# Channel sums of a state-space mixer: from image rows on chip instead of a read-back from DRAM

## The chip, the cores and the metric

The kernel runs on one core of one Trainium2 chip. The metric is device time in microseconds (us) of one execution. A core has TensorE (PE: matrix products and transposes), VectorE (DVE), ScalarE (ACT), GpSimd (POOL) and SyncE (SP, which here only issues DMAs). Each engine works through its own instructions in the order in which the program gave them; semaphores tie the engines and the DMAs together. An instruction that waits holds up everything behind it on its engine.

## The reference

Two layers run on two images of 128 channels and 64x64 pixels. Layer 0 has four deformable convolutions (60 taps, each gathers four neighbours per pixel), a fusing product and a small expert network. Layer 1 has a state-space mixer and another expert network. What the change touches is the channel and position attention in the mixer:

```python
xz = jnp.einsum('ed,bdhw->behw', in_proj_w, hidden_states)
xz = lax.conv_general_dilated(xz, dwconv_w, ..., feature_group_count=2 * DI)   # 5x5, one per channel
x, z = (xz[:, :DI], xz[:, DI:])                  # DI = 256 channels each, L = 4096 pixels
avg = jnp.mean(x, axis=-1, keepdims=True)        # per channel, over all pixels
mx = jnp.max(x, axis=-1, keepdims=True)
x = jax.nn.sigmoid(ca_branch(avg) + ca_branch(mx)) * x
stats = jnp.concatenate([jnp.mean(z, axis=1, ...), jnp.max(z, axis=1, ...)], axis=1)   # per pixel
att = lax.conv_general_dilated(stats, sa_conv_w, ...)
z = jax.nn.sigmoid(att) * z
```

After it come a causal convolution along the pixels, a scan (256 channels x 16 states x 4096 steps per image) and an output product. `ca_branch` is a product with a 16x256 matrix, a SiLU, and a product with a 256x16 matrix.

## The kernel before

**The large stages.** One instruction stream does layer 0 and the mixer for both images. The instructions of all engines are in an order that Python generators write out by hand. First come the 480 taps of image 0, then the 480 taps of image 1 (`sample`, line 755): per tap four indirect gathers on POOL (L748) into one of six buffers `v`, a weighting on DVE (L789, L791, L792), four transposes on PE into `pst`, a copy on ACT (L796) and the product on PE (L816), which is issued two taps late. Then comes the scan of image 0 (`scan`, line 1568), then that of image 1, then the last expert network. A scan has 256 units per image (8 pieces `k` of 512 pixels x 2 halves x 16 states). A unit is a scan on DVE (L1685) of `da` (ACT, L1604) and `db` (POOL, L1597, from a row `bcb` that SP loads, L1615), a transpose on PE (L120, `ht`), a weighting on DVE (L1631) and an adding transpose on PE (L1642).

**What runs beside them.** Everything between the taps of an image and its scan (fusing product, expert network, the mixer's convolutions) is a chain of generators, `after(b)`. For image 0 it runs beside the taps of image 1: each tap takes two steps of it (L806). For image 1 it runs beside the scan of image 0: each unit earns one credit, and steps are taken until it is spent (L1710). A step is charged what it yields, 0.11 where it yields nothing. So steps that are added or taken away shift all later side work against the units. When the side work of image 1 has ended, the remaining units of image 0 run alone, with half of the weighting on ACT, and from piece 7 on with the preparation of image 1's first piece (`prepare`, four of its steps per unit).

**The mixer's convolutions** (`convs`, line 1186) go through four groups `o` of 128 channels, in the order 2, 3, 0, 1: 2 and 3 are z, 0 and 1 are x. In each group comes first the input product (L1251, 22 steps charged 0.45; ACT copies the result to `X`). Then for two parts of 64 channels: the 5x5 convolution as products with position matrices (L1264, 8 steps; ACT copies to `Y`), and the image rows (L1286: PE transposes of `Y`; ACT copies into `img`; SP writes `img` to the DRAM tensors `xsd` or `zsd`). An `img` tile has 128 partitions, 64 channels of the upper and the same 64 channels of the lower half of each patch; four of them, `py` = 0 to 3, make up the 64 channels. They have three buffers, in a tag `io` that other tiles share. Copies are not issued at once: `later` holds them back by two steps, `last` issues what is held.

**The sums, before.** For z, DVE reduces all of `Y` over its 64 channels, once by adding (L1304) and once by the maximum (L1306), with one step between. For x, `channel_stats` (line 1337) loads the channels back from `xsd`, 128 partitions x 512 pixels at a time (L1340, 256 KB, 16 loads per image, in the `io` buffers), and reduces each load twice (L1343, L1344). The loads of the first 128 channels run beside the input product of group 1 (`at == 2`, L1311), those of the second after everything else (L1313). Then `channel_attention` (line 1347) combines eight partial results per channel and does the two small products (L1359, L1366), two sigmoids and the scaling of the taps' weights (L1370).

Of the kernel before, what the change touches and what calls it, by code (L numbers as in the profile page):

```python
# [10 lines left out]
F32 = mybir.dt.float32  # L11
I32 = mybir.dt.int32
AF = mybir.ActivationFunctionType
ALU = mybir.AluOpType
AX = mybir.AxisListType
# [4 lines left out]
P = 128  # L20
# [3 lines left out]
N = H * W  # L24
# [6 lines left out]
NG = NT // GT  # L31
# [1057 lines left out]
PH, PW = 8, 6  # L1089
# [3 lines left out]
NPOS = PH * PW  # L1093
CG = 128
YG = 64
# [36 lines left out]
class L1Conv:  # L1132
# [11 lines left out]
    def constants(self):  # L1144
        nc, d, wp = self.env.nc, self.env.d, self.wp

        def load(name, shape, src=None):
            t = wp.tile(shape, F32, name="w_" + name)
            nc.sync.dma_start(out=t, in_=d[name] if src is None else src)
            return t  # L1150

        self.c1w = load("conv1d_w", [P, 2, 4])
        self.c1b = load("conv1d_b", [P, 2])
        self.xpw = load("x_proj_w", [P, 2, 40])
        self.dtb = load("dt_proj_b", [P, 2])
        self.A = load("A_log", [P, 2, DS])
        self.D = load("D", [P, 2])
        self.fc1 = load("ca_fc1_w", [P, 2, 16])
        self.fc2 = load("ca_fc2_w", [16, 256])
        self.saw = load("sa_conv_w", [14, 1])  # L1160
        yield
        self.sqb = wp.tile([P, len(SQUARES)], F32, name="sqb")
        for i, (_, t, _) in enumerate(SQUARES):
            nc.vector.memset(self.sqb[:, i : i + 1], t)
        nc.scalar.activation(self.A, self.A, AF.Exp)
        nc.vector.tensor_scalar(self.A, self.A, -1.0, None, ALU.mult)
        self.xsd = [self.dp.tile([256, N], F32, name=f"xsd{b}", tag=f"xsd{b}") for b in range(B)]
        self.zsd = [self.dp.tile([256, N], F32, name=f"zsd{b}", tag=f"zsd{b}") for b in range(B)]
        self.att = [self.dp.tile([2, N + 6], F32, name=f"att{b}", tag=f"att{b}") for b in range(B)]
        self.sad = [self.dp.tile([1, N], F32, name=f"sad{b}", tag=f"sad{b}") for b in range(B)]  # L1170
        self.w1 = [wp.tile([P, 2, 4], F32, name=f"w1_{b}") for b in range(B)]
        for b in range(B):
            for s in range(2):
                nc.sync.dma_start(out=self.att[b][s : s + 1, 0:3], in_=self.env.zero[0:1, 0:3])
                nc.sync.dma_start(out=self.att[b][s : s + 1, N + 3 :], in_=self.env.zero[0:1, 0:3])
            yield
# [9 lines left out]
    def convs(self, b, sp, pp):  # L1186


        env, nc, d = self.env, self.env.nc, self.env.d
        bank = lambda shape, name: pp.tile(shape, F32, name=name, tag="m")  # L1190
# [9 lines left out]
        def last():  # L1200
            while held:
                for f in held.popleft():
                    f()
                yield 0.3
            yield
# [3 lines left out]
        hs, own, tm, beside = self.hs[b], {}, {}, deque()  # L1209
# [30 lines left out]
            matrices()  # L1240
        yield 0.5
        zst = sp.tile([NPATCH, 2, 256 // YG, NPOS], F32, name="zst", bufs=1)
        st = sp.tile([P, 2, 2, NG], F32, name="st8", bufs=1)
        for at, o in enumerate(ORDER):
            X = sp.tile([KP, CG, NPATCH], F32, name="X", bufs=1)
            for p0 in range(0, NPATCH, 4):
# [9 lines left out]
            for part in range(CG // YG):  # L1256
# [23 lines left out]
                for py in range(PH // 2):  # L1280
                    img = sp.tile([P, NI, W], F32, name="img", tag="io", bufs=3)
                    for x0, nx in ((0, 4), (4, 2)):
                        ps = bank([P, nx, NPATCH], "ps3")
                        for x in range(nx):
                            two = Y[:, py * PW + x0 + x, :, :].rearrange("p h c -> p (h c)")
                            nc.tensor.transpose(ps[:, x, :], two, env.ident[:NPATCH, :NPATCH])  # L1286
                        nj = NJ if x0 + nx <= W - PW * (NJ - 1) else NJ - 1
                        to = view(img, x0, [(W, NI), (PW, nj), (1, nx)])
                        todo = [copy(to, ps.rearrange("p x (i j) -> p i j x", j=NJ)[:, :, 0:nj, :])]
                        if x0:  # L1290
                            for h in range(2):
                                row = dst[:, py + h * PH // 2, :, :]
                                todo.append(functools.partial(nc.sync.dma_start, out=row, in_=img[h * YG : (h + 1) * YG]))
                        later(*todo)
                        yield 0.45
                    if py == 1:
                        matrices()
                        if part == 0:
                            weights(at + 1)
                yield from last()  # L1300
                if not x_half:
                    n = lo // YG
                    zs = zst[:, :, n, :].rearrange("p k (h s) -> p k s h", h=2)
                    nc.vector.tensor_reduce(zs[:, 0, :, :], Y, AX.X, ALU.add)  # L1304
                    yield
                    nc.vector.tensor_reduce(zs[:, 1, :, :], Y, AX.X, ALU.max)  # L1306
                yield
            if at == 1:
                beside.append(self.position_attention(b, zst, sp, bank, room))
            if at == 2:  # L1310
                beside.append(mixed([self.channel_stats(b, 0, g, st, sp) for g in range(NG)], 2))  # L1311

        yield from mixed([self.channel_stats(b, 1, g, st, sp) for g in range(NG)], 3)  # L1313
        yield from self.channel_attention(b, st, sp, bank)

    def norm(self, b, x, hn, g, sp, bank, banks, act):
# [17 lines left out]
        nc.scalar.copy(hs[:, 0 : NJ - 1, rows, PW : PW + 4], hs[:, 1:NJ, rows, 0:4])  # L1334
        yield

    def channel_stats(self, b, half, g, st, sp):
        nc = self.env.nc
        xs = sp.tile([P, 512], F32, name="xst", tag="io", bufs=3)
        nc.sync.dma_start(out=xs, in_=self.xsd[b][half * P : (half + 1) * P, g * 512 : (g + 1) * 512])  # L1340
        for _ in range(3):
            yield
        nc.vector.tensor_reduce(st[:, half, 0, g : g + 1], xs, AX.X, ALU.add)  # L1343
        nc.vector.tensor_reduce(st[:, half, 1, g : g + 1], xs, AX.X, ALU.max)  # L1344
        yield

    def channel_attention(self, b, st, sp, bank):

        nc = self.env.nc
        one = lambda shape, name: sp.tile(shape, F32, name=name, bufs=1)  # L1350
        amp = one([P, 2, 2], "amp")
        for half in range(2):
            nc.vector.tensor_reduce(amp[:, half, 0:1], st[:, half, 0, :], AX.X, ALU.add)
            nc.vector.tensor_reduce(amp[:, half, 1:2], st[:, half, 1, :], AX.X, ALU.max)
            nc.vector.tensor_scalar(amp[:, half, 0:1], amp[:, half, 0:1], 1.0 / N, None, ALU.mult)
        yield
        p1 = bank([16, 2], "p1")
        for half in range(2):
            nc.tensor.matmul(p1, self.fc1[:, half, :], amp[:, half, :], start=half == 0, stop=half == 1)  # L1359
        r1, r2 = one([16, 2], "r1"), one([16, 2], "r2")  # L1360
        nc.scalar.activation(r1, p1, AF.Sigmoid)
        nc.vector.tensor_tensor(r2, r1, p1, ALU.mult)
# [753 lines left out]
```

## Time and profile before

| what | value |
|---|---|
| median of three runs | 7552.04 us (7550.52 to 7557.68) |
| the profiled execution: its own time | 7555.38 us |
| the profiled execution: its span | 7553.5 us |
| busy DVE / PE / POOL / ACT in the span | 5857.3 / 5203.1 / 5036.0 / 2135.7 us |
| mean granted TensorE clock | 0.825 |
| mixer's convolutions of image 0, beside image 1's taps | 4216 to 5411 us |
| last tap of image 1 | 5722 us |
| scan of image 0 | 5764 to 6743 us |
| mixer's convolutions of image 1, beside it | 6198 to 6666 us |

The span runs from the first to the last instruction. A busy share is a mean over stages with different limits, so each stage has to be read for itself. In a list of waits a line names the instruction that waited, what ended the wait, and the total in us, the number of waits and the longest. In a line of the timeline stand the start and the duration in us, engine, line, operation, output and input; the number in brackets is the idle time of the engine just before, and what ended it. In a table of stretches stand busy us and, in brackets, the number of instructions of each engine, then the granted clock, the share of DMA time and GB/s.

### The profile page before, as it was taken

What the parts mean: (1) busy time and instruction counts of PE and PEld (TensorE: products, weight loads), DVE (VectorE), ACT (ScalarE), POOL (GpSimd) and SP (SyncE); (2) the same over time, 40 slices, a digit from 0 to 9 for tenths busy, and PEclk for the clock granted to TensorE, in tenths of its full rate; (3) what the DMA queues carried; (4) which work ended last, traced back from release to release, by engine and by line L of the source; (5) the groups of instructions that cost most, each with busy time, mean ns of one, the idle gap of its engine ahead of it and who ended that gap; (6) DMA issues with size and microseconds to landing.
All of it is one profiled execution on the core that took longest, in us unless ns stands there. A gap on an engine that the chain in (4) does not pass through costs nothing.

```text
span 7553.5 us, 71416 instructions
## 1 busy us (share of the span) xinstructions
PE 5203.1 (69%) x22497; PEld 3269.2 (43%) x22497; DVE 5857.3 (78%) x6710; ACT 2135.7 (28%) x4194; POOL 5036.0 (67%) x5062
## 2 busy tenths in 40 slices
PE   4666777777767675766666766666556788867668
PEld 3344444444444442333323444434223567755444
DVE  6878888888888887788888877777775787678782
ACT  2211111111111111311111121211114675667870
POOL 4666777777777777777777776677775445567850
PEclk7887887878888887888888887877777898888899
DMA  7886777776777767877777777687775334555444
GB/s 239 253 275 206 216 210 218 211 220 208 220 213 219 214 210 251 281 232 212 224 217 216 217 232 235 207 251 216 228 208 188 118 103 129 138 155 163 153 148 156
DMA packets 667316, 1550.02 MB, mean 205 GB/s; under 512 B 181668, under 2 KB 230988, under 8 KB 666940
## 3 DMA queue, kind: packets, MB, share of 16 engines
q0 software_dynamic: 307200, 1006.88, 44.2%
q1 hardware_dynamic: 332540, 492.98, 20.9%
q10 hardware_dynamic: 27200, 45.59, 1.6%
q8 instruction: 182, 2.98, 0.2%
q14 instruction: 194, 1.59, 0.1%
HBM read 1436.70 MB, written 110.84 MB: 205 GB/s over the span
## 4 chain that ended last, share of the span: by engine, by line
PE 39%; issue 18%; another core or an unknown queue 13%; DVE 8%; POOL 7%; ACT 7%; DMA 3%; SPq 1%; ACTq 0%; DVEq 0%; POOLq 0%
PE out L816 17%; PE pst L120 6%; POOL v L748 5%; PE po L437 4%; POOL db L1597 2%; DVE h L1685 2%; ACT st L796 2%; DVE v L789 2%; PE ps L1264 2%; PE pfo L892 1%; PE ps L1251 1%; PE px L1045 1%; PE ht L120 1%; DVE q L1557 1%
## 5 line engine op out<-in xcount | busy, mean ns | idle before, releaser
L748 POOL DMA_INDIRECT v<-table,idx x3840 | 4042.1, 1053 | 1629.6 <-issue 1047.7
L789 DVE TENSOR_TENSOR v<-v,pw 128x2048 f32<-128x2048 f32 x960 | 2192.0, 2283 | 611.3 <-DMA v<-table,idx 429.3
L816 PE MATMUL out<-st,regw 128*128 128x512 f32 x3840 | 2234.7, 708 | 225.3 <-issue 164.1
L796 ACT COPY st<-pst 128x512 f32<-128x512 f32 x960 | 556.9, 586 | 4402.2 <-remote 2198.4
L120 PE MATMUL pst<-ident,v 128*128 128x128 f32 x3840 | 721.3, 313 | 1061.0 <-issue 874.3
L791 DVE TENSOR_TENSOR v<-v 128x1024 f32<-128x1024 f32 x960 | 1177.3, 1226 | 33.0
L816 PEld LDWEIGHTS out<-st,regw 128*128 128x128 f32 x3840 | 790.7, 228 | 887.1 <-issue 813.5
L120 PEld LDWEIGHTS pst<-ident,v 128*128 128x128 f32 x3840 | 517.3, 161 | 1431.5 <-issue 1214.8
L1597 POOL TENSOR_TENSOR db<-du,bcb 128x512 f32<-128x512 f32 x512 | 670.9, 1311 | 493.5 <-DVE h L1685 382.8
L1685 DVE TENSOR_TENSOR_SCAN h<-da,state,db 128x512 f32<-128x512 f32 x512 | 651.8, 1273 | 77.9 <-ACT da L1604 48.0
L792 DVE TENSOR_TENSOR v<-v 128x512 f32<-128x512 f32 x960 | 664.2, 692 | 33.0
L120 PE MATMUL ht<-ident,h 128*128 128x128 f32 x2048 | 357.6, 303 | 221.0 <-ACT w L1633 150.9
L437 PE MATMUL po<-wa,win 128*128 128x147 f32 x2112 | 386.4, 306 | 104.7 <-issue 101.9
L437 PEld LDWEIGHTS po<-wa,win 128*128 128x128 f32 x2112 | 339.4, 204 | 226.6 <-issue 226.2
L1604 ACT ACTIVATE da<-delta,w_A_log 128x512 f32<-128x512 f32 x512 | 357.7, 699 | 262.6 <-DVE h L1685 258.0
L120 PEld LDWEIGHTS ht<-ident,h 128*128 128x128 f32 x2048 | 259.8, 155 | 345.4 <-ACT w L1633 223.0
L1631 DVE TENSOR_TENSOR w<-ht,ct 128x128 f32<-128x128 f32 (+2 forms) x512 | 232.8, 455 | 181.9 <-PE ht L120 179.8
L1251 PE MATMUL ps<-ipw,hs 128*120 128x128 f32 x1408 | 212.9, 309 | 181.7 <-ACT X L1198 92.8
L1642 PE MATMUL py<-ident,w 128*128 128x128 f32 x2048 | 337.2, 295 | 0.0
L1251 PEld LDWEIGHTS ps<-ipw,hs 128*120 128x120 f32 x1408 | 196.3, 212 | 235.9 <-ACT X L1198 109.7
L1642 PEld LDWEIGHTS py<-ident,w 128*128 128x128 f32 x2048 | 272.4, 155 | 23.3 <-issue 23.0
L1264 PE MATMUL ps<-tm,X 120*88 120x48 f32 x2048 | 214.9, 278 | 87.2 <-ACT Y L1198 42.2
(327 smaller groups left out, 5289.5 us busy)
## 6 DMA issues: line engine op xcount, KB each, us to landing
bcb<-bc SPq DMA_DIRECT2D x512, 256.0 KB
regw<-in_regw SPq DMA_DIRECT2D x192, 640.0 KB
v<-table,idx POOLq DMA_INDIRECT x3840
yd<-ys ACTq DMA_DIRECT2D x128, 256.0 KB
yc<-yd SPq DMA_DIRECT2D x16, 2048.0 KB
wt<-in_weight SPq DMA_DIRECT2D x32, 1024.0 KB
tm<-pos SPq DMA_DIRECT2D x32, 720.0 KB
pos<-zero SPq DMA_DIRECT2D x48, 240.0 KB
```

The lines of the kernel that those rows point to most:

```text
L120: nc.tensor.transpose(ps[:, j, :], s, ident)
L437: m()
L748: self.env.nc.gpsimd.indirect_dma_start(out=v[:, j, :], out_offset=None, in_=self.table[b], in_offset=bass.IndirectOffsetOnAxis(ap=idx[:, ...
L789: nc.vector.tensor_tensor(v4, v4, w, ALU.mult)
L791: nc.vector.tensor_tensor(up, up, v4[:, :, 2:4, :], ALU.add)
L792: nc.vector.tensor_tensor(v4[:, :, 0, :], v4[:, :, 0, :], v4[:, :, 1, :], ALU.add)
L796: nc.scalar.copy(st, pt.rearrange("p j t -> p (j t)"))
L816: nc.tensor.matmul(self.out[half], self.regw[t // CH][:, t % CH, half * P : (half + 1) * P], st, start=first, stop=last,)
L1251: nc.tensor.matmul(ps[:, k, :], patch, own[o], start=True, stop=True)
L1597: nc.gpsimd.tensor_tensor(dbs[u], pieces[k]["du"][:, half, :], rows.pop(u), ALU.mult)
L1642: nc.tensor.matmul(py[k][:, j * P : (j + 1) * P], w[:, j, :], env.ident, is_transpose=True, start=False, stop=n == DS - 1 and j == GT - 1,)
L1685: nc.vector.tensor_tensor_scan(hs[u], das.pop(u), dbs.pop(u), state[:, half, n : n + 1], ALU.mult, ALU.add)
```

## The change

The sums of x come from the `img` tiles while they are on the chip: each of the four `img` tiles of a part is reduced over all its pixels, by adding and by the maximum, into one column of `st`. These two instructions are held in a list `sums` and issued together with the first copy of the next `img` tile, or at the end of the part. The 32 loads and `channel_stats` are gone. Since an `img` tile has the upper and the lower half of the patches on different partitions, `channel_attention` has to add partitions 0 to 63 to 64 to 127: it transposes the sums on PE, copies them with ACT, combines the halves along the free axis on DVE, and transposes back. The first small product then takes four parts of 64 channels instead of two of 128, so its matrix `fc1` is loaded in two DMAs. The sums of z over channels are made in two halves of `Y`, with a step after each of the four instructions.

```diff
-        self.fc1 = load("ca_fc1_w", [P, 2, 16])
+        self.fc1 = wp.tile([YG, 2, 2, 16], F32, name="w_ca_fc1_w")
+        for part in range(2):
+            nc.sync.dma_start(out=self.fc1[:, :, part, :], in_=d["ca_fc1_w"][part * YG : (part + 1) * YG, :, :])
...
-        st = sp.tile([P, 2, 2, NG], F32, name="st8", bufs=1)
+        st = sp.tile([P, 2, 4, PH // 2], F32, name="st8", bufs=1)
+        sums = []
...
+                        if x_half and not x0:
+                            todo, sums = todo + sums, []
+                        if x0 and x_half:
+                            for i, op in enumerate((ALU.add, ALU.max)):
+                                into = st[:, i, lo // YG, py : py + 1]
+                                sums.append(functools.partial(nc.vector.tensor_reduce, into, img, AX.XY, op))
...
                 yield from last()
+                for f in sums:
+                    f()
+                sums = []
                 if not x_half:
...
-                    nc.vector.tensor_reduce(zs[:, 0, :, :], Y, AX.X, ALU.add)
-                    yield
-                    nc.vector.tensor_reduce(zs[:, 1, :, :], Y, AX.X, ALU.max)
+                    for i, op in enumerate((ALU.add, ALU.max)):
+                        for q in range(0, NPOS // 2, NPOS // 4):
+                            cut = slice(q, q + NPOS // 4)
+                            nc.vector.tensor_reduce(zs[:, i, cut, :], Y[:, cut, :, :], AX.X, op)
+                            yield
                 yield
...
-            if at == 2:
-                beside.append(mixed([self.channel_stats(b, 0, g, st, sp) for g in range(NG)], 2))
-
-        yield from mixed([self.channel_stats(b, 1, g, st, sp) for g in range(NG)], 3)
...
-    def channel_stats(self, b, half, g, st, sp):
...
-        amp = one([P, 2, 2], "amp")
-        for half in range(2):
-            nc.vector.tensor_reduce(amp[:, half, 0:1], st[:, half, 0, :], AX.X, ALU.add)
-            nc.vector.tensor_reduce(amp[:, half, 1:2], st[:, half, 1, :], AX.X, ALU.max)
-            nc.vector.tensor_scalar(amp[:, half, 0:1], amp[:, half, 0:1], 1.0 / N, None, ALU.mult)
+        amp, both = one([P, 2, 4], "amp"), []
+        for i, op in enumerate((ALU.add, ALU.max)):
+            nc.vector.tensor_reduce(amp[:, i, :], st[:, i, :, :], AX.X, op)
+        yield
+        pt = bank([4, 2, P], "pst")
+        for i in range(2):
+            nc.tensor.transpose(pt[:, i, :], amp[:, i, :], env.ident)
+        yield
+        rows = one([4, 2, P], "amr")
+        nc.scalar.copy(rows, pt)
+        yield
+        four = one([4, 2, YG], "amf")
+        for i, op in enumerate((ALU.add, ALU.max)):
+            nc.vector.tensor_tensor(four[:, i, :], rows[:, i, 0:YG], rows[:, i, YG:], op)
+        yield
+        pa = bank([YG, 4, 2], "psa")
+        for i in range(2):
+            nc.tensor.transpose(pa[:, :, i], four[:, i, :], env.ident[0:4, 0:4])
+        yield
+        amc = one([YG, 4, 2], "amc")
+        nc.vector.tensor_scalar(amc[:, :, 0], pa[:, :, 0], 1.0 / N, None, ALU.mult)
+        nc.vector.tensor_copy(amc[:, :, 1], pa[:, :, 1])
         yield
         p1 = bank([16, 2], "p1")
-        for half in range(2):
-            nc.tensor.matmul(p1, self.fc1[:, half, :], amp[:, half, :], start=half == 0, stop=half == 1)
+        for n in range(4):
+            nc.tensor.matmul(p1, self.fc1[:, n // 2, n % 2, :], amc[:, n, :], start=n == 0, stop=n == 3)
```

## The prediction

> **What bounds the kernel now.** I read the page's busy shares first. No engine is full over the whole span, so the answer lies in stages, and the change touches two: the mixer's convolutions of image 0 beside the taps of image 1, and those of image 1 beside the scan of image 0.
>
> ```profile
> span 7553.5 us, 71416 instructions
> PE 5203.1 (69%) x22497; PEld 3269.2 (43%) x22497; DVE 5857.3 (78%) x6710; ACT 2135.7 (28%) x4194; POOL 5036.0 (67%) x5062
> ```
>
> Second, the table of stretches in the first stage: a stretch with convolutions, and the last one, in which the taps run without them. The POOL count is gathers, four to a tap.
>
> ```profile
> 5130.00:5300.00 170.00, 112.37 (x574) 75.41 (x574) 121.39 (x89) 30.12 (x67) 119.34 (x115) 0.79 0.74 215
> 5411.00:5700.00 289.00, 162.99 (x430) 76.21 (x431) 231.39 (x173) 33.06 (x57) 212.17 (x200) 0.78 0.70 208
> ```
>
> That is 170/115*4 = 5.91 us per tap beside convolutions and 289/200*4 = 5.78 us without. The same table gives 87 gathers in 124 us (5.70) and 79 in 111 us (5.62) where the sums of x run. The stage goes at the pace of POOL's gathers, and side work hardly matters. The timeline of DVE at the end of image 0's side work, and POOL's waits in that stretch (5382 to 5412):
>
> ```profile
> 5385.81 0.69 DVE L792 TENSOR_TENSOR v<-v 128x512 f32<-128x512 f32 x1
> 5409.33 0.14 DVE L1362 TENSOR_TENSOR r<-r,p 16x2 f32<-16x2 f32 x1 [22.83 <-ACT r L1361]
> ...
> POOL v L748 <- remote: 4.6, 2, 3.1
> ```
>
> DVE stood 22.8 us behind the channel attention, and POOL lost 4.6 us: the six `v` buffers take up most of it.
>
> Third, DVE's waits in the second stage (5764 to 6740), and its timeline at the two sums of x.
>
> ```profile
> DVE w L1631 <- PE ht L120: 125.3, 74, 8.2
> DVE h L1685 <- ACT da L1604: 18.2, 13, 4.3
> DVE st L1343 <- DMA xst<-xsd: 17.9, 3, 9.8
> ...
> 6537.24 0.66 DVE L1631 TENSOR_TENSOR w<-ht,ct 128x512 f32<-128x512 f32 x1
> 6547.73 0.69 DVE L1343 TENSOR_REDUCE st<-xst 128x1 f32<-128x512 f32 x1 [9.82 <-DMA xst<-xsd]
> 6548.33 0.68 DVE L1344 TENSOR_REDUCE st<-xst 128x1 f32<-128x512 f32 x1
> 6548.92 1.27 DVE L1685 TENSOR_TENSOR_SCAN h<-da,state,db 128x512 f32<-128x512 f32 x1
> ...
> 6639.68 0.66 DVE L1631 TENSOR_TENSOR w<-ht,ct 128x512 f32<-128x512 f32 x1
> 6647.56 0.69 DVE L1343 TENSOR_REDUCE st<-xst 128x1 f32<-128x512 f32 x1 [7.22 <-DMA xst<-xsd]
> ```
>
> The next scan stands behind the waiting reduction, and the other engines behind the scan: this wait is on the path. The chain that ended last runs through it in both places, at the second so:
>
> ```profile
> 6638.48 0.62 SPq L1198
> ...
> 6640.45 4.12 DMA xsd<-img
> 6644.68 2.85 DMA xst<-xsd
> 6647.56 0.69 DVE st L1343
> ```
>
> I numbered the units by the scans' starts. In the image-row phases a unit takes 1.77 us with DVE without a gap; in an input-product phase 2.83 us (units 128 to 138, 6308.76 to 6339.87, PE busy 28.64 of 32 us).
>
> **The change, part by part: image 1, beside the scan.**
>
> 1. *First 128 channels, units 189 to 203.* They took 6532.51 to 6582.97, 50.46 us for 15 units. Eight loads of four steps at 0.11 go, 3.52 units of credit. The remaining 11.5 run like the input product of units 128 to 138: 11.5*2.83 = 32.5. The 3.5 units left over run after the side work's end at 1.51 us (units 226, 228, 229): 5.3. Together 37.8, so -12.7: the waits (9.8+0.9) and a little of the 16 reductions at 0.59 us start to start, most of which stood beside PE's work anyway.
>
> 2. *Second 128 channels and the attention, units 222 to 225.* 6638.49 to 6665.87 is 27.4 us. The 3.52 credits and their reductions go. What stays is half a unit and one with the attention, 0.9+1.8 us, and the attention's chain, 3.5 us before (6662.38 to 6665.87). The chain gains two transposes on PE (L120: four in 0.6 to 1.12 us, so 0.3 to 0.56), a copy on ACT between the 0.30 us of 160 and the 0.47 of 352 elements, two DVE operations (0.14 to 0.17 each), two small transposes, two small DVE operations and two more products (L1359: two in 0.38). That is some 2 us, of which 0.9 lie beside the sigmoid's table load of 1.28 us, which set the pace there: +1.1 (0.5 to 2.5). So 7.3 remain, plus 5.3 for the leftover units: 12.6 instead of 27.4, -14.8.
>
> 3. *The 32 reductions come back in the four image-row phases.* 128x512 each as before, 0.59 us: +19.0. Two of the phases have DVE gaps of 1.9 and 2.3 us (DVE waiting for `ht`), which take up 3; the other two have none. New is a wait: a reduction needs the last ACT copy of its `img`, issued one step (0.45) earlier, and ACT makes it after `da`, which waits for the same unit's scan. If both fall into one unit, DVE has 0.6 us of weighting to do while ACT needs 0.69+0.3 to 0.47 and sometimes a copy before; a wait of 0.4 to 1.1 us, in about half of 16 images, +5 (0 to 9). Behind it on DVE stands the next scan. I take +21 (14 to 26). The next user of the `img` buffer (ACT's copy three tiles later) waits for the reductions too; those are 2.7 units older, so nothing.
>
> 4. *Sums of z.* 16 reductions of 3.34 us become 32 (both images). Two of the old ones lengthen a unit from 1.77 to 8.29 us (unit 127), 3.26 each for 3072 elements; with 0.59 for 512 that is 1.04 ns per element and 0.06 us per instruction: +0.5 for image 1. The extra credits (12*0.11, and 5*0.11 of the attention) are 1.9 units at 1.77 and not at 1.51: +0.5. A unit's end falls between the parts more often, so PE gets on: -0 to -3, I take 1. Sum 0 (-2 to +1).
> The Trainium skill, page "VectorE: DVE Perf Modes", section "Rules for kernel authors", speaks against splitting (keep the number of operations low), and its section on the errata measures a fixed term of about 150 cycles, 0.16 us. An estimate by that page would be +1.3 us for image 1 in place of the trace's 0.5.
>
> 5. *SP.* 16 loads (0.32 us of issue each) leave the queue, and with them the waits ahead of the `bcb` rows: POOL's `db` waited 26.6 us in 12 pieces for rows between 6480 and 6700. That lies inside points 1 and 2 and is not counted again. `fc1` in two loads adds one issue near the start, at most 0.6 us, hidden by queue idle time (bound 0 to 0.6).
> On a store and a load in turn, the skill's page "DMA: Bandwidth & Descriptors", section "Anatomy of one DMA", has a fixed cost of about 2.0 us each, on the GpSimd path. By that page two such trips would be 8 us, and the waits saved about half. The trace, from SP and beside other traffic, shows 4.12 and 2.85 us, and DVE waits of 9.8 and 7.2.
>
> Image 1: -12.7-14.8+21+0 = -6.5, bounds -16 to +1 (points 2, 3 and 4 at their ends).
>
> **Image 0, beside the taps.** The same edits, 47 steps fewer (64 less 12 less 5), so the side work ends 23 taps earlier. Those taps go from 5.6 to 5.7 us each to 5.78: no gain, up to +3. 4.2 MB less traffic at a DMA share of 0.7 to 0.8: up to 5 us if gathers were held by it; their waits do not say so. The new waits of DVE on ACT (16 images) and the attention's four turns through PE or ACT instead of two hold up the weighting behind them; the cover is the `v` buffers. If the cover is used up each costs POOL up to the 4.6 us above. I take 0, bounds -6 and +28 (six such pauses: four parts, two turns).
>
> **Sum.** The profiled execution took 7555.4 (span 7553.5 and 1.9 around it), 3.3 above the median of 7552.0. Without the change's terms that is the base; -6.5+0 gives 7548.9, at the median 7545.5. I predict 7546.
>
> **The rivals.** About 0.2%, 15 us, is what a measurement of this kernel can tell from no change.
> *Better cover.* The reductions disappear in `ht` waits (DVE waited 125.3 us for `ht` in the scan) and ACT is always early: point 3 at +14, the chain at 0.5, and -6 in image 0. -16-6: 7530. For it: 74 such waits; against it: 1.77 us units without gaps just where the reductions land.
> *DVE tied to ACT beside the gathers* (the other side). Each part's sums make DVE wait for an ACT that lags: ACT waits of up to 15.6 us occur in this stage. It decides once pauses follow each other faster than DVE's spare 1.5 us per tap (5.8 less 4.2) refills the buffers. Six pauses of 4.6: +28, with image 1's -6.5: +21, 7573. Against it: the 22.8 us pause cost so little.
> *A new last wait for the old one.* `bcb` rows or ACT's copies take the place of the 17.9 us, as a reduction now waits on ACT in every image: points 1 and 2 give only 20 in place of 27.5. +1: 7553.
>
> **How the numbers follow.** Likeliest -6.5: 0.48; new last wait: 0.13; better cover: 0.24; DVE tied to ACT: 0.15. Faster by over 0.2%: the better cover and a little of the likeliest, 0.26. Slower: the tied DVE, 0.15. Within: 0.59. The range leaves out the outer parts of both: 7526 (the better cover and 4 more) to 7566 (half of the tied DVE's cost). The likeliest alone: 7537 to 7555.
>
> **What would show it.** No `xst` in DVE's waits; units 191 and 222 without their 12.9 and 12.6 us. Image-row units of groups 0 and 1 near 3 us instead of 1.77, and DVE waits "st <- ACT img". Side work of image 1 ending near unit 220, not 225. Taps beside convolutions still 5.7 to 5.9 us. Wrong, if the last tap of image 1 moves by over 10 us, if the waits on ACT's copies pass 10 us beside the scan, or if freed units run slower than 1.51 us.

## The result, and the profile after

Measured side by side on one chip, the changed kernel takes 7571.55 us (median of 14 runs, 7562.89 to 7589.72), the kernel before 7557.39 us (14 runs, 7543.96 to 7574.12). The ratio is 1.002, with a 95% interval of 1.0013 to 1.0027: 14 us slower, 0.2%. The forecast of 7546 us was on the wrong side, and the value lies above its range (7526 to 7566). How much slower is less certain than the interval says: measured again in a later series, the same two kernels differ by 4 us (-6 to +15), as the run `after_again` below shows.

The page of the profile after, its span and busy engines:

```profile
span 7566.5 us, 71453 instructions
PE 5238.3 (69%) x22513; PEld 3295.4 (44%) x22513; DVE 5858.9 (77%) x6726; ACT 2143.4 (28%) x4206; POOL 5077.7 (67%) x5062
```

DVE's busy time is the same as before to 2 us, and the span is 13.0 us longer. So nothing more is computed on DVE; something waits longer.

First the taps. The table of stretches after the change, for the taps before the side work of image 0's convolutions begins, and with it (busy us and instructions of PE, PEld, DVE, ACT, POOL, then clock, DMA share, GB/s):

```profile
2800.00:4216.00 1416.00, 895.73 (x2752) 447.94 (x2752) 1163.60 (x1267) 270.07 (x468) 1044.87 (x977) 0.83 0.73 231
4216.00:5722.00 1506.00, 983.11 (x4034) 583.65 (x4032) 1146.99 (x875) 261.56 (x522) 1065.91 (x1015) 0.79 0.73 220
```

POOL's instructions here are its gathers, 977 and 1015. The kernel before made 978 and 1016 in the same stretches, one more in each. The last gather of image 1 starts at 5709.8 instead of 5706.5. The taps lose 3.3 us at most.

Then DVE's waits in the scan of image 0 after the change (5768 to 6746):

```profile
DVE w L1649 <- PE ht L120: 133.0, 75, 7.2
...
DVE xr L1755 <- DMA xr<-x: 13.8, 2, 10.9
DVE st L1200 <- ACT img L1200: 9.3, 7, 4.2
...
DVE st L1311 <- ACT img L1205: 2.4, 2, 1.5
```

The wait for `xst` (17.9 us) is gone. New is `st <- ACT img`: with 0.9 us more at L1205 it makes 12.6 us in 11 waits. And DVE now waits 10.9 us, not 8.2, for a transfer that the change does not touch: `xr`, which belongs to image 0's output product, `project(6)`.

The starts of the scans (L1685 before, L1703 after), counted from unit 0, put this into places. Differences of the two profiles, in us:

| stretch | before | after | difference |
|---|---|---|---|
| start of the span to unit 0 | 5764.7 | 5768.6 | +3.9 |
| units 0 to 128 | 544.1 | 541.9 | -2.2 |
| units 128 to 226 (image 1's convolutions) | 357.1 | 359.7 | +2.6 |
| units 226 to 239 (`project(6)`, `prepare(8)`) | 48.6 | 55.2 | +6.6 |
| unit 239 to the end | 839.0 | 841.2 | +2.1 |

The first two and the last scatter by as much in the profiles of the experiments below, with the change and without it (units 0 to 128: 537.9 to 544.5; unit 239 to the end: 839.0 to 843.3, but for `hold_234`, which moves work into that stretch; start of the span to unit 0: 5414.8 to 5448.6). So two places are left, and they are what the experiments are about: image 1's convolutions, which were forecast to win 6.5 us and lose 2.6, and thirteen units after them, for which nothing was forecast.

In the first place a reduction stands behind a copy that ScalarE makes late. From the timeline after, unit 179:

```profile
6503.91 0.69 ACT L1558 ACTIVATE v<-pd,w_dt_proj_b 128x512 f32<-128x512 f32 x1 [1.23 <-PE pd L1554]
...
6504.69 1.06 ACT L1562 ACTIVATE e<-v 128x1024 f32<-128x1024 f32 x1
...
6505.78 1.06 ACT L1563 ACTIVATE e<-e 128x1024 f32<-128x1024 f32 x1
6506.75 0.99 ACT L1200 COPY img<-ps 128x352 f32<-128x352 f32 x3
...
6507.42 1.28 DVE L1200 TENSOR_REDUCE st<-img 128x1 f32<-128x512 f32 x2 [4.17 <-ACT img L1200]
...
6508.61 1.28 DVE L1703 TENSOR_TENSOR_SCAN h<-da,state,db 128x512 f32<-128x512 f32 x1
```

ACT works through the exponentials of the next piece's preparation before it comes to the copies of `img`; DVE stands 4.17 us at the reduction, and the next scan behind it. The forecast had ACT do only `da` and a copy or two there. Ahead of the second longest wait, in unit 207, ACT loads a table (1.28 us) and makes two `da` before the copies:

```profile
6600.53 1.28 ACT L1622 ACT_TABLE_LOAD   x1
6601.82 1.30 ACT L1622 ACTIVATE da<-delta,w_A_log 128x512 f32<-128x512 f32 x2
...
6603.74 1.28 DVE L1200 TENSOR_REDUCE st<-img 128x1 f32<-128x512 f32 x2 [2.58 <-ACT img L1200]
```

The other nine waits are of 0.41 to 1.47 us and make 5.9 us together.

The second place is unit 230, 17.16 us instead of 11.04. From the timeline before:

```profile
6674.28 0.42 DVE L1631 TENSOR_TENSOR w<-ht,ct 128x256 f32<-128x256 f32 x1 [0.51 <-PE ht L120]
...
6674.52 1.95 PE L1727 MATMUL po<-ow,zc 128*128 128x128 f32 x16
...
6676.50 0.37 SPq L1504 DMA_DIRECT2D zc<-zsd  x1
...
6677.90 0.43 SPq L1722 DMA_DIRECT2D xr<-x  x1
...
6681.35 1.26 POOL L1463 TENSOR_TENSOR zc<-zc,sab 128x512 f32<-128x512 f32 x1 [6.10 <-DMA sab<-sad]
...
6682.93 0.69 DVE L1737 TENSOR_TENSOR xr<-xr,po 128x512 f32<-128x512 f32 x1 [8.23 <-DMA xr<-x]
```

And the same instructions after:

```profile
6678.22 3.60 PE L1479 MATMUL pc<-xc,wd 128*128 128x512 f32 x8
...
6682.29 0.42 DVE L1649 TENSOR_TENSOR w<-ht,ct 128x256 f32<-128x256 f32 x1 [4.00 <-PE ht L120]
...
6682.53 1.95 PE L1745 MATMUL po<-ow,zc 128*128 128x128 f32 x16
...
6684.51 0.37 SPq L1522 DMA_DIRECT2D zc<-zsd  x1
...
6686.87 0.42 SPq L1740 DMA_DIRECT2D xr<-x  x1
...
6690.13 1.26 POOL L1481 TENSOR_TENSOR zc<-zc,sab 128x512 f32<-128x512 f32 x1 [15.69 <-DMA sab<-sad]
...
6693.59 0.69 DVE L1755 TENSOR_TENSOR xr<-xr,po 128x512 f32<-128x512 f32 x1 [10.87 <-DMA xr<-x]
```

The side work of image 1 now ends in unit 220 instead of 225, so `prepare(8)`, the preparation of image 1's first piece, begins earlier, and eight of its `pc` products (3.60 us) stand on PE ahead of `project(6)`'s product `po`. The load of `zc` for the next part of `prepare(8)` needs the buffer that `po` still reads, so SP issues it only when `po` is done, and in SP's queue the load of `xr` stands behind it. Of the 6.1 us that unit 230 grows, 3.48 are `po`'s: it starts 5.5 us after the unit's scan (6677.03) instead of 2.0 us (6672.50). Another 0.96 are SP's: between the loads of `zc` and `xr` it issues three `bcb` rows instead of one, so `xr` follows 2.36 us behind `zc` and not 1.40. The last 1.69 are the load's own: DVE's addition comes 6.72 us after its issue instead of 5.03.

### The profile page after: what moved, and what is told of

Its sections match the earlier page's. It is cut to its first block, busy times and chain, and to the rows that moved or that the text cites. A ratio compares the mean times of both kernels' runs of the same rounds, so it can differ in the third digit from the quotient of the medians.

```text
span 7566.5 us, 71453 instructions
## 1 busy us (share of the span) xinstructions
PE 5238.3 (69%) x22513; PEld 3295.4 (44%) x22513; DVE 5858.9 (77%) x6726; ACT 2143.4 (28%) x4206; POOL 5077.7 (67%) x5062
## 5 line engine op out<-in xcount | busy, mean ns | idle before, releaser
L1703 DVE TENSOR_TENSOR_SCAN h<-da,state,db 128x512 f32<-128x512 f32 x512 | 652.7, 1275 | 77.0 <-ACT da L1622 47.9
L1267 PEld LDWEIGHTS ps<-tm,X 120*88 120x88 f32 x2048 | 215.8, 191 | 114.2 <-ACT Y L1200 41.4
```

The source lines that it names most:

```text
L1267: nc.tensor.matmul(ps[:, c, :], X[:, ch + c0 + c, :], t[:, :, c0 % TG + c], start=True, stop=True)
L1703: nc.vector.tensor_tensor_scan(hs[u], das.pop(u), dbs.pop(u), state[:, half, n : n + 1], ALU.mult, ALU.add)
```

## The experiments

Theory A: the loss lies beside image 1's scan, in two parts: DVE's waits on ScalarE's copies, and unit 230. Theory B: image 0, DVE tied to ScalarE beside the gathers. Theory C: the split sums over channels, or credits moved by units.

The experiments ran in three later series, in which the kernel before takes 7211.15, 7218.32 and 7237.17 us and not 7557, so they are taken to be on other chips than the first comparison. Ratios are to the kernel before in the same series. The first and the third series are on the same chip by its number and yet 26 us apart, so times of different series aren't compared. A stretch of the scan is compared with any other profile; the kernel before has one profile, the first one. The stretches of each profile, in us, with the ratio of times:

| kernel | 128-226 | 226-239 | unit 0 to end | ratio (95%) |
|---|---|---|---|---|
| before | 357.1 | 48.6 | 1788.8 | 1 |
| after (first chip) | 359.7 | 55.2 | 1797.9 | 1.002 (1.0013-1.0027) |
| `after_again` | 362.4 | 55.3 | 1803.7 | 1.0006 (0.9992-1.0021) |
| `hold` | 343.5 | 56.1 | 1780.9 | 0.9996 (0.9987-1.0006) |
| `xr_act` | 369.8 | 53.9 | 1805.3 | 1.0007 (0.9995-1.002) |
| `hold_xr` | 345.0 | 54.6 | 1777.7 | 0.9983 (0.9974-0.9993) |
| `pad` | 363.5 | 47.8 | 1795.6 | 1.0001 (0.9989-1.0013) |
| `hold_226` | 343.7 | 47.0 | 1774.9 | 0.9979 (0.9969-0.9988) |
| `hold_234` | 345.0 | 21.8 | 1779.1 | 0.999 (0.9981-0.9999) |
| `img0_only` | 354.4 | 48.1 | 1786.6 | 0.9992 (0.9983-1.0001) |
| `img1_only` | 366.7 | 55.0 | 1802.4 | 1.0011 (1.0001-1.0021) |
| `no_read` | 329.8 | 48.3 | 1764.3 | 0.9951 (0.9933-0.997) |
| `no_sums` | 330.7 | 55.6 | 1770.4 | 0.9967 (0.9957-0.9978) |
| `z_whole` | 364.4 | 55.4 | 1806.0 | 1.0008 (0.9996-1.002) |

**The sums one step later** (`hold`). The two reductions of an image are issued with the second copy of the next image instead of the first; what is left at the end of a part goes with the first copy of the next stage.

```diff
-                        if x_half and not x0:
+                        if x_half and x0:
                             todo, sums = todo + sums, []
...
                 yield from last()
-                for f in sums:
-                    f()
-                sums = []
...
-                later(copy(X[:, :, p0 : p0 + 4], ps.rearrange("p k c -> p c k")))
+                later(copy(X[:, :, p0 : p0 + 4], ps.rearrange("p k c -> p c k")), *sums)
+                sums = []
...
```

> The changed kernel with each image's sum and maximum issued one step later: behind the copy of the next image row instead of behind its own, so that DVE finds ScalarE's copy of that image done. Theory A (two costs beside image 1's scan: DVE waits of 12.6 us on ScalarE's copies, and project(6)'s unit, 17.2 us for 11.0): DVE's waits on the copies of img and st from 6480 to 6672 us fall from 12.6 to 3 us or less, unit 226 starts 6 to 10 us earlier than in the changed kernel, unit 230 keeps about 17 us; total 4 to 8 us above the kernel before. Theory B (the loss is image 0's, DVE tied to ScalarE beside the gathers): the scan of image 0 starts 3 us or more earlier than in the changed kernel, and image 1's shorter waits leave the total where the start of the scan put it. Theory C (the split sums over channels or credits moved by units): the total stays at 12 to 16 us above the kernel before, with shorter waits.

DVE's waits in units 175 to 230 (6155 to 6336) of this kernel:

```profile
DVE w L1650 <- PE ht L120: 37.6, 21, 7.2
...
DVE st L1200 <- ACT img L1200: 0.9, 1, 0.9
```

The waits on the copies go from 12.6 us to 0.9, and units 128 to 226 take 343.5 us: 16.2 less than after, and 13.6 less than before (10.9 less than `img0_only`, which leaves image 1 as it was). That is more than the waits. The rest is in the first line: the same list over the same units after the change has `w <- PE ht` at 44.2 us, 6.6 more. Of these, 5.1 us stand in unit 213 (5.8 us after, 0.7 here), where the granted clock differs. Table of stretches after, units 207 to 209, units 210 to 212 and unit 213:

```profile
6598.80:6612.40 13.60, 10.54 (x81) 7.45 (x80) 9.27 (x13) 7.77 (x17) 8.95 (x12) 0.99 0.62 160
6612.40:6620.60 8.20, 8.20 (x40) 6.37 (x39) 7.22 (x10) 4.18 (x7) 3.65 (x6) 0.50 0.77 166
6620.60:6630.20 9.60, 9.60 (x60) 8.48 (x59) 3.77 (x6) 4.76 (x8) 2.41 (x4) 0.56 0.29 108
```

And the same units with the sums later:

```profile
6269.30:6279.00 9.70, 9.00 (x77) 6.92 (x75) 7.89 (x11) 7.28 (x17) 8.35 (x12) 1.00 0.46 119
6279.00:6287.30 8.30, 8.00 (x67) 6.14 (x67) 8.30 (x12) 5.83 (x11) 4.27 (x6) 1.00 1.04 258
6287.30:6291.90 4.60, 4.60 (x43) 4.07 (x44) 3.85 (x5) 3.40 (x6) 2.88 (x4) 1.00 0.79 279
```

Where DVE waits for the copies, PE runs dry (busy 10.54 of 13.6 us, against 9.00 of 9.7), and in the following 17.8 us its clock is 0.50 to 0.56 instead of 1.00. Unit 213, which PE fills, then takes 9.54 us for 4.59. The other profiles agree. In units 176 to 226 the mean granted clock is 0.76 to 0.81 in the six profiles in which DVE waits 11.7 to 12.9 us for the copies, and 0.85 to 0.87 in the five in which the change is made without these waits (0.9 us or none: the four `hold` kernels and `no_sums`); the matrix products there, 1203 to 1234 records, keep PE busy for 160 to 170 us in the six and 147 to 151 in the five. That PE's idle time is the link between the waits and the clock is read from the order of the rows and was not tried by itself. Unit 230 stays at 17.07 us, as theory A has it: the two parts are independent. The total was expected 4 to 8 us above the kernel before; 0.9996 is 3 us below it (-9 to +4), so that was missed, to the good side.

**The load of `xr` past SP's queue** (`xr_act`, and with the sums later `hold_xr`).

```diff
-        nc.sync.dma_start(out=xr, in_=self.x2[b][:, k * GT : (k + 1) * GT, :])
+        queue = nc.scalar if (b, k) == (0, N // LC - 2) else nc.sync
+        queue.dma_start(out=xr, in_=self.x2[b][:, k * GT : (k + 1) * GT, :])
```

> The changed kernel with one edit: the load of xr of project(6) of image 0 is issued from ScalarE's queue instead of SyncE's, where a zc load that waits for a buffer stands ahead of it. Theory A: DVE's wait of 10.87 us on the DMA of xr in unit 230 goes to 3 us or less, the unit from 17.2 to 8 to 11 us; total 5 to 8 us above the kernel before (6 to 9 below the changed kernel). If the wait on TensorE's po, not the queue, sets the unit, it stays near 17 us and the total at +14. Theory B (image 0) and theory C (the split sums) both leave the total at 12 to 16 us above the kernel before, whatever unit 230 does.

> Both edits: the sums one step later, and project(6)'s xr load from ScalarE's queue. Theory A: the gains add, 12 to 18 us below the changed kernel, so 4 us below to 2 us above the kernel before. Theory B: only what the scan of image 0 starts earlier, total 6 to 14 us above the kernel before. Theory C: 10 us or more above it.

Unit 230 of `xr_act` takes 15.04 us, not 8 to 11. Its timeline:

```profile
6333.51 0.33 ACTq L1741 DMA_DIRECT2D xr<-x  x1
...
6338.78 1.95 PE L1746 MATMUL po<-ow,zc 128*128 128x128 f32 x16
...
6340.76 0.37 SPq L1522 DMA_DIRECT2D zc<-zsd  x1
6340.77 0.69 DVE L1756 TENSOR_TENSOR xr<-xr,po 128x512 f32<-128x512 f32 x1 [1.80 <-PE po L1746]
...
6345.68 1.26 POOL L1481 TENSOR_TENSOR zc<-zc,sab 128x512 f32<-128x512 f32 x1 [14.90 <-DMA sab<-sad]
...
6348.32 1.28 DVE L1703 TENSOR_TENSOR_SCAN h<-da,state,db 128x512 f32<-128x512 f32 x1 [6.87 <-POOL state L1712]
```

The load is issued 5.3 us before `po` starts, and DVE's addition waits only 1.80 us, for `po`. But a second wait hangs on the same late `zc` load: POOL stands 14.90 us at `zc*sab`, the scan needs POOL's copy of `state` (L1712), and that stands behind. POOL had waited there before this edit too (15.69 us); now its wait is the one that ends last, in place of DVE's. So the queue is only one of two ways by which a late `po` reaches the scan, and the part of theory A that blamed the queue alone fell.

The total (+5 us by the ratio) came out as expected, but not for the reason: in units 176 to 192, long before its edit, this profile took 79.6 us against 72.5 and 73.0 of two profiles of the unedited changed kernel. The timeline of PE there, `xr_act` first:

```profile
6176.71 2.58 PE L1267 MATMUL ps<-tm,X 120*88 120x48 f32 x16 [3.94 <-ACT Y L1200]
...
6180.81 4.83 PE L1267 MATMUL ps<-tm,X 120*88 120x48 f32 x32
```

and `after_again`, the same instructions:

```profile
6214.38 2.58 PE L1267 MATMUL ps<-tm,X 120*88 120x48 f32 x16 [3.96 <-ACT Y L1200]
...
6218.49 3.34 PE L1267 MATMUL ps<-tm,X 120*88 120x48 f32 x32
```

The idle time just before them is the same (3.94 and 3.96 us), and 32 products take 4.83 us in one and 3.34, then 2.89 in the other; the granted clock over units 186 to 188 is 0.54 and 1.00. No edit lies ahead of this place, so it is chance, some 7 us of it.

`hold_xr` takes 0.9983 of the time before, some 12 us less, where -4 to +2 had been expected: 345.0 us in units 128 to 226, like `hold`, and 54.6 us after that. By these stretches nearly all of its gain is the sums'. The totals of the same series put it 10 us below `hold`; the two profiles show only 3 of them in the scan (1777.7 and 1780.9), and the rest stays open.

**The old start of `prepare(8)`** (`pad`; `hold_226`; `hold_234`). In `pad` 47 empty steps follow image 1's channel attention, which brings `prepare(8)` back to unit 226. The other two hold it back directly, on top of the later sums:

```diff
-            if k + 1 < B * NK and k + 1 not in pieces and (k != NK - 1 or not rest.todo):
+            if k + 1 < B * NK and k + 1 not in pieces and (k != NK - 1 or not rest.todo and u >= 226):
```

> The changed kernel with 47 empty steps behind image 1's channel attention, so that its first piece, prepare(8), begins near unit 226 again, where the kernel before begins it, and not in unit 224. Theory A: the zc load stands no longer ahead of project(6)'s xr load by as much; unit 230 goes back from 17.2 to 10 to 12 us, nothing else of image 1's scan moves by more than 2 us; total 6 to 10 us above the kernel before. If unit 230 is slow for another reason than prepare(8)'s early start, it stays near 17 us. Theories B and C leave the total at 12 to 16 us above the kernel before.

> The sums one step later (as in the run of that edit alone, whose scan from its first unit to the end of the span took 1780.9 us, with 56.1 us from unit 226 to unit 239), and prepare(8) added no earlier than unit 226, without empty steps. Theory A (project(6) pays for prepare(8) having begun before it in the side work, by the zc load whose buffer project(6) still reads): units 226 to 239 take 47 to 49 us, unit 230 about 10.5; the scan's stretch 1772 to 1776 us; total 8 to 16 us below the kernel before. Rival (the xr load's place in SyncE's queue alone sets unit 230): units 226 to 239 stay near 55 us and the total near the kernel before.

> As the run with unit 226, but prepare(8) is added no earlier than unit 234, behind all of project(6). Theory A: no zc load stands ahead of project(6)'s loads and po comes right behind the scan's own matmuls, so unit 230 falls from about 10.5 to 3 to 6 us; prepare(8)'s own units (3 of 4 to 10 us) come back unchanged between units 234 and 247; from unit 226 to unit 252 4 to 8 us less than with unit 226; total 12 to 22 us below the kernel before. Rival (unit 230's time is project(6)'s own: the load, po and the addition): unit 230 stays at 9 to 11 us and nothing is gained over unit 226.

`pad`: unit 230 takes 10.29 us and units 226 to 239 take 47.8, as before the change, with SP's queue as it was. So it is the start of `prepare(8)` that cost 6.6 to 7.4 us. (The empty steps cost 1.3 us of their own: units 221 to 225 take 1.77 us each instead of 1.51.) The total, 1.0001, is lower than the expected +6 to +10 us, but its interval (-8 to +9) holds most of that. `hold_226`: unit 230 9.45 us, the thirteen units 47.0, the time 0.9979 (0.9969 to 0.9988) of before, some 15 us: within what theory A gave, and faster than both kernels.

`hold_234` shows the mechanism bare. Timeline of its unit 230:

```profile
6320.77 1.95 PE L1746 MATMUL po<-ow,zc 128*128 128x128 f32 x16
...
6322.75 0.69 DVE L1756 TENSOR_TENSOR xr<-xr,po 128x512 f32<-128x512 f32 x1 [0.97 <-PE po L1746]
...
6323.36 1.28 DVE L1704 TENSOR_TENSOR_SCAN h<-da,state,db 128x512 f32<-128x512 f32 x1
```

With no `zc` load ahead the unit takes 3.19 us: 6.3 of the 9.45 are `prepare(8)`'s. But nothing is won. Units 226 to 252 take 69.0 us, against 67.1 of `hold_226`: `prepare(8)` by itself lengthens seven units (239 to 245, to 2.6 to 9.4 us), and the expectation that its own units come back unchanged was wrong. It seems that part of its work had stood in the shadow of unit 230's wait. The total is 0.999, a gain of 7 us where 12 to 22 were expected.

**One image alone** (`img0_only`, `img1_only`). Each takes the new way, with the split sums of z, for one image and the old for the other; `fc1` is loaded in the fitting layout before each.

```diff
+        new = b == 0
...
+        st = sp.tile([P, 2, 4, PH // 2] if new else [P, 2, 2, NG], F32, name="st8", bufs=1)
...
-                        if x0 and x_half:
+                        if new and x0 and x_half:
...
+        if new:
+            yield from self.channel_attention(b, st, sp, bank)
+        else:
+            yield from mixed([self.channel_stats(b, 1, g, st, sp) for g in range(NG)], 3)
+            yield from self.channel_attention_old(b, st, sp, bank)
```

> The changed way for image 0 alone (sums and maxima from the image rows, beside the taps); image 1 reads back from DRAM as before. Theory A (all of the loss lies beside image 1's scan): the scan's stretch as before (1788 to 1792 us; 357 us from unit 128 to 226, 48.5 us from 226 to 239), total within 5 us of the kernel before. Theory B (image 0, DVE tied to ScalarE beside the gathers, carries a part): total 6 us or more above the kernel before, with the gathers' stretch longer by it.

> The changed way for image 1 alone; image 0 reads back from DRAM as before. Theory A: the scan's stretch as in the changed kernel (1796 to 1800 us; 359 to 362 us from unit 128 to 226, 55 us from 226 to 239), total 5 to 12 us above the kernel before. Theory B: the scan's stretch is longer all the same, but the total is at least 4 us below that of the fully changed kernel, whose ratio was 1.002 (+14 us).

Image 0 alone: 0.9992 (0.9983 to 1.0001), that is -6 us (-12 to +1), where up to 5 either way had been expected. Its scan's stretch is that of before to 2 us. Nothing is slower: theory B falls. Image 1 alone: 1.0011, +8 us (+1 to +15), within theory A's 5 to 12, its thirteen units 55.0 us. Theory B's sign for this run, at least 4 us below the +14 of the full change, is met by the number too; it has no weight, because the full change itself came out at +4 in a later series and the interval holds both. Its units 128 to 226 take 366.7 us, over the 359 to 362 expected, and its scan 1802.4, over 1796 to 1800; most of the surplus is the clock at units 186 to 188 again (0.61; 14.12 us for these units, 9.42 in `after_again`).

**What is removed and what comes back** (`no_read`, `no_sums`). The first is the kernel before without the loads of `xst` and their reductions, the second the changed kernel without the 32 reductions of `img`. In both the sums and maxima of x are zero, so the scaling of x is computed from nothing.

```diff
+        nc.vector.memset(st, 0.0)
...
-        nc.sync.dma_start(out=xs, in_=self.xsd[b][half * P : (half + 1) * P, g * 512 : (g + 1) * 512])
...
-        nc.vector.tensor_reduce(st[:, half, 0, g : g + 1], xs, AX.X, ALU.add)
-        nc.vector.tensor_reduce(st[:, half, 1, g : g + 1], xs, AX.X, ALU.max)
```

```diff
+        nc.vector.memset(st, 0.0)
...
-                                sums.append(functools.partial(nc.vector.tensor_reduce, into, img, AX.XY, op))
+                                pass
```

> The kernel before without its read-back: the loads of xst and their 64 reductions are left out (sums and maxima of x are zero), the empty steps of these helpers and the attention stay. It prices what the change removes. Theory A (the removal was priced rightly, at 27.5 us for image 1's two places): unit 191 and unit 222 go from 12.9 and 12.6 to under 3 us, and units 128 to 226 take 328 to 336 us instead of 357; total 20 to 30 us below the kernel before. Rival (the read-back was mostly cover for other work, and its waits are replaced by DVE's wait on TensorE's ht): 343 us or more for these units, total less than 15 us below.

> The changed kernel without the 32 sums and maxima of image rows (st is set to zero; sums and maxima of x are left out); transposes, copies and attention stay. Theory A (the sums cost their DVE time and 12.6 us of waits, and with them the matmuls that come late behind the wait): units 128 to 226 take 325 to 335 us instead of 359.7; unit 230 stays near 17 us; total 10 to 20 us below the kernel before. Rival (the image rows' time is TensorE's and ScalarE's, and the reductions stand beside it): 345 us or more.

In units 128 to 226 the read-back is worth 357.1-329.8 = 27.3 us, and the sums 359.7-330.7 = 29.0. The two kernels without either differ by 0.9 us (329.8 and 330.7), so the other edits come out even here (6.5 us less in units 128 to 176, 7.4 more in 176 to 226): -27.3+0.9+29.0 = +2.6. Both stretches came out as theory A has them. The totals fell by more than expected, 35 us (22 to 48) for 20 to 30, and 24 us (16 to 31) for 10 to 20; single times of the kernel before lie between 7192.77 and 7253.45 us in this series, so the stretches say more here than the totals.

**The sums of z in one piece** (`z_whole`), and the changed kernel once more (`after_again`).

```diff
-                        for q in range(0, NPOS // 2, NPOS // 4):
-                            cut = slice(q, q + NPOS // 4)
+                        for q in range(1):
+                            cut = slice(0, NPOS // 2)
```

> The changed kernel with each sum and maximum of Y over channels in one instruction, as before the change. Theory A (the split costs nothing that can be seen): units 96 to 176 within 2 us of the changed kernel's 384.7, the scan's stretch 1796 to 1800 us, total 8 to 16 us above the kernel before. Theory C (the split, by the work it moves to other units, carries a part): units 96 to 176 5 us or more shorter, total within 6 us of the kernel before.

> The changed kernel itself, unchanged, beside the three others on their chip. All theories: scan's stretch 1796 to 1802 us, units 226 to 239 55 us, total 8 to 16 us above the kernel before.

Units 96 to 176 take 292.0 us with the sums whole, and 284.7 and 287.0 in the two profiles of the changed kernel (the 384.7 of the expectation is a slip of 100 us). So the expected 2 us was wrong, but to the other side of theory C: the split takes 5 to 7 us off these units. All profiles say the same: 283.9 to 289.3 us with the split for image 1, 292.0 to 295.7 without. These profiles don't show it given back later either (units 176 to 226 take 189.4 us whole, 188.8 and 189.2 split; the whole scan 1806.0, over the 1796 to 1800 expected, against 1797.9 and 1803.7). The total doesn't resolve it: 1.0008, +6 us (-3 to +14), under the 8 to 16 us expected, against `after_again`'s 1.0006. Theory C falls. `after_again` is 1.0006, under the expected 8 to 16 us, with an interval (-6 to +15) that holds them; its scan stretch of 1803.7 us lies just above the range given, its thirteen units at 55.3.

## Why the prediction was wrong

- **Points 1 and 2 (the read-back, -12.7 and -14.8): right in the sum.** Both waits for `xst` went, units 191 and 222 fell to 2.96 and 1.51 us, the side work ended in unit 220, and the freed units ran at 1.51 us up to 228 (but for 227, 2.10 before and after). Together 27.5 was forecast, and leaving the read-back out measures 27.3. The attention's chain is one of the terms that no run priced by itself: it was counted at 4.6 us and took 6.5 (6656.05 to 6662.55), with a scan of 1.3 us inside it.
- **Point 3 (the 32 reductions come back, +21, 14 to 26): mis-sized, and the first step that failed.** Leaving them out measures 29.0. The term in it that was wrong is the new wait, +5 (0 to 9): 12.6 us. The reasoning counted ACT's `da` and one or two copies ahead of the copy of `img`, and for the nine ordinary waits that was about right (5.9 us). It left out what else ACT does there: the next piece's exponentials (4.17 us at unit 179) and a table load (2.58 us at unit 207). And it had no term for the clock, which in units 176 to 226 is lower in every profile with these waits than in any without them in the changed kernel: 6.6 us more of `ht` waits, 5.1 of them in unit 213. Issued one step later the reductions wait 0.9 us, and these units take 13.6 us less than before the change. So the gain of the change was there, and its place in DVE's queue lost it.
- **Point 4 (sums of z, 0, -2 to +1):** in units 96 to 176 the split gains 5 to 7 us by `z_whole`, more than the range allowed; what of it reaches the total isn't resolved.
- **Point 5 (SP, not counted):** it put POOL's waits for `bcb` rows down to the sixteen loads. The kernel without the loads, `no_read`, has these waits all the same: 30.3 us in units 176 to 239, where the kernel before has 26.6 and the changed kernel 6.7. So the loads weren't their cause. And the point looked only at what leaves the queue, not at what moves up in it.
- **What no step priced, and what failed most in the end:** the units after the side work. The forecast ended image 1's work at unit 220 and let units 226, 228 and 229 run at 1.51 us, which they did but for 229 (1.74). It never asked what an earlier end starts earlier. `prepare(8)` starts with it, gets ahead of `project(6)` on PE and in SP's queue, and makes unit 230 6.1 us longer, units 226 to 239 6.6.
- **Image 0 beside the taps (0, -6 to +28): right.** DVE did wait for ACT there, 44.4 us in 8 waits for copies of `img` (4216 to 5722), and the last gather moved only 3.3 us; changed alone, image 0 is not slower.
- **The rivals.** "DVE tied to ACT beside the gathers" (7573) has the right total by luck and the wrong place: DVE was tied to ACT beside the scan. "A new last wait for the old one" (7553) names the right mechanism, a reduction that waits on ACT, though in 11 of 16 images; it charged it to points 1 and 2, which held, and it has nothing of unit 230. "Better cover" was wrong as the change was written, and the two repairs give two thirds of it (0.9979, some 15 us, for 22).
- **Of the signs it named,** the waits on ACT's copies passed 10 us beside the scan, which it gave as one that would prove it wrong.

The sum by the two places that stay from profile to profile: +2.6 in place of -6.5, and +6.6 in place of nothing: +9.2 in the scan, 9.1 of them seen between unit 0 and the end (1797.9-1788.8). The other 3.9 of the span lie ahead of unit 0, and no run ties them to the change: that part of the cause stays open.

## What to carry to other kernels

When work is taken away from a side stream, list what the stream starts when it ends, and what that will overtake on each engine and in each DMA queue: a load that waits for a buffer holds up everything behind it in the queue, and its consumer holds up everything behind it on its engine, so moving one of the two past the other changes little. When a reduction is tied to a producer on another engine, count all that stands in that engine's queue ahead of the producer, not just its regular work; one step more of distance cost nothing here and was worth 16 us. And before calling a wait 5 us, ask whether it also leaves the matrix engine idle, and look at the granted clock behind it.

## What had not been expected of the hardware

- Waits of DVE go with a slower PE: a granted clock of 0.50 and 0.56 over 17.8 us behind a stretch in which PE was busy 10.54 of 13.6 us, and 1.00 in the same units without these waits.
- The same instructions with the same idle time just ahead of them (3.94 and 3.96 us) ran at 0.54 in one profile and 1.00 in another. The clock records of all 14 profiles hold no values but 0.50 and 1.00, so 0.54 is a mean over both. The Trainium skill, page "TensorE: Matmul & The Clock Gate", section "What's actually happening", tells of a window of about 3.4 us that runs freely and does not start with the kernel's work, with a half and a full clock; that agrees with the two values here. That such a window makes the chance isn't shown by a run.
- The two kernels took 7557 and 7572 us in the first comparison and 7211 to 7246 us in the later series. The scan's stretch of the changed kernel is the same to 0.4% (1797.9 and 1803.7 us); the whole difference lies ahead of unit 0 (5768.6 and 5448.6 us), where the gathers are.
